# A 1x1 convolution of two by two blocks, made by seven products instead of eight

## The chip, the cores and the metric

The kernel runs on one core of a Trainium2 chip. Time is device time in microseconds (us) from start to end of one execution. TensorE (PE) multiplies, VectorE (DVE) and ScalarE (ACT) work elementwise, GpSimd (POOL) and SyncE (SP) mostly issue transfers. Each engine takes its instructions strictly in the order in which the program lists them, and waits at an instruction until what it needs is there. PE writes its results to PSUM, which the kernel uses as banks that it hands round ("big", 128 x 1024 numbers each), and reads its operands from SBUF. ACT computes silu and exp from tables; going from one function to the other needs an ACT_TABLE_LOAD.

## The reference, cut to what matters

```python
t = cbs(x, cv1_w, cv1_bn, 0)             # 1x1 convolution, batch norm, silu
ys = [t[:, :C], t[:, C:]]                # C = 256 channels of 32x32
for i in range(2):                       # two bottlenecks
    yi = ys[-1]
    z = cbs(yi, m_cv1_w[i], m_cv1_bn[i], 1)              # 3x3
    z = bot_attention(z, m_qkv_w[i], m_rw[i], m_rh[i])   # 4 heads of 64
    z = silu(bn_eval(conv2d(z, m_cv2_w[i], 0), m_cv2_bn[i]))   # this is m2
    ys.append(yi + z)
return cbs(concatenate(ys, axis=1), cv2_w, cv2_bn, 0)
```

The input (8 images of 512 channels) goes through a group norm first, and is added to the result at the end. All is 32-bit. m2 is the 1x1 convolution from 256 to 256 channels behind attention, with its batch norm, silu and the addition of `yi`.

## The kernel before, in words

The eight images are worked off in four pairs (p = 0 to 3, images a and b), each pair through cv1, the two bottlenecks (n = 0 and 1) and cv2. A 1x1 convolution of 256 channels on 1024 positions is a product of two by two blocks: two blocks of 128 input channels (k), two of 128 output channels (oc), two halves of 512 positions (half). One product of a 128x128 weight with a 128x512 block is two matmul instructions in the trace. Many convolutions of the kernel are already made in Strassen's way (in Winograd's form), by seven products and sums of blocks: the projection to q, k and v (`project_strassen`, L939) with its products named `11`, `s1`, `12`, `s4`, `s2`, `s3`, `22` and its sums on DVE, and pieces of cv1 (`nxt.begin`, `rest`, `adds`, `finish`).

`m2` (L1328 to L1345) isn't: it makes eight products (L1336), each pair of them adding up in PSUM, four silus straight from PSUM (L517, `t<-m_ps`), and four additions of `yi` on DVE (L1344). It is called 16 times: for each pair, bottleneck and image. Its weights `m2_sb` for both bottlenecks are loaded once at the start.

The calls for image a, which the change touches, stand at three kinds of places:

- *direct*: p = 0, n = 0. m2 runs, and behind it the rest of cv1 and a projection made in the plain way.
- *more*: n = 0 of p = 1 and 2. m2 stands between the pieces `nxt.rest(0)` to `nxt.rest(3)` of the next image's cv1 (x_ps, L1828; copies L1839 and L1842), and image b's projection follows.
- *middle*: n = 1 of every pair, and n = 0 of p = 3; five places. m2 is called inside image b's projection, by `middle()`, between its products `s2` and `s3`.

At a middle place the order of before is: `end.spread()` and `end.scale()` (L1195 scales attention's output z, two instructions on DVE; the second is the block that m2's products of k = 1 wait for), m2's eight products, the projection's `s3` and `22` (L958 for q and k, L964 for v), their additions on DVE (L1033 to L1050), and then attention: four groups of logits (L1082), each into a bank of PSUM that an exp (L1086) empties, then the products with v (L1119), and sums of the exps on DVE (L1100, L1103). In n = 1 of p = 1 and 2 `middle()` also calls `nxt.finish()`, which puts six silus of the next cv1 (`ypad`, `y_half`) on ACT behind m2's four, and `nxt.keep()`. Behind all of these `exp_table()` (L532, a table load and a tiny activation `spare`) is put behind the last silu, and the exps follow. DVE's and ACT's order is the order in which the program issues, apart from `tc.issue_after`, which puts an instruction behind a named one.

## Time and profile before

| | us |
|---|---|
| median of 3 runs (lowest, highest) | 2207.69 (2206.78, 2208.18) |
| the profiled execution | 2206.25 |
| its span in the profile | 2204.8 |
| PE busy | 2176.4 |
| DVE busy | 1817.5 |
| ACT busy | 1094.1 |

The profiled execution took 2206.25 us, of which the profile's span covers 2204.8; the other 1.45 lie around it. A busy time is the time in which an engine's instructions ran, summed up. In the lists of instructions each row is: start, duration, engine, line, operation, output <- inputs, shapes, how many, and in brackets the idle time ahead of it and what ended it.

### The profile page before, as it was taken

How to read it: one execution, taken by the hardware profiler on the slowest of the kernel's cores; microseconds unless marked ns; L12 is line 12 of the kernel's file. 1: busy time of each engine (PE TensorE's matmuls, PEld its weight loads, DVE VectorE, ACT ScalarE, POOL GpSimd, SP SyncE). 2: the span in 40 equal slices, each digit the busy share in tenths (PEclk: the TensorE clock that was granted, in tenths of full speed). 3: DMA queues.
4: the chain of work that ended last, by engine and by line, in shares of the span. 5: the costliest groups of instructions: out<-in, count | busy, mean ns of one | idle time of the engine just before them, and what ended most of it. 6: DMA issues, size and time to landing. Idle time of an engine off the chain costs nothing.

```text
span 2204.8 us, 40989 instructions
## 1 busy us (share of the span) xinstructions
PE 2176.4 (99%) x16546; PEld 1117.9 (51%) x16546; DVE 1817.5 (82%) x2996; ACT 1094.1 (50%) x1320; POOL 220.9 (10%) x393
## 2 busy tenths in 40 slices
PE   7999999999999999999999999999999999999998
PEld 3653438343484444734458443564346834383436
DVE  8988879878978688986897868997788877897677
ACT  7454553554225666366314676455622465336543
POOL 4322210000210000000012000000002100000001
PEclk9999999999999999999999999999999999999999
DMA  9954447212583323612159141542126811261224
GB/s 276 323 159 143 163 149 262 84 52 74 153 287 95 118 84 127 208 51 77 57 135 330 33 165 38 184 140 78 59 68 170 301 30 45 92 204 32 76 59 116
DMA packets 135529, 291.93 MB, mean 132 GB/s; under 512 B 33732, under 2 KB 61376, under 8 KB 134308
## 3 DMA queue, kind: packets, MB, share of 16 engines
q1 hardware_dynamic: 102708, 201.01, 27.4%
q0 software_dynamic: 32624, 88.23, 13.6%
q8 instruction: 132, 2.16, 0.4%
q14 instruction: 65, 0.53, 0.1%
HBM read 219.58 MB, written 69.60 MB: 131 GB/s over the span
## 4 chain that ended last, share of the span: by engine, by line
PE 87%; DVE 8%; DMA 2%; issue 1%; ACT 1%; POOL 0%; SPq 0%; DVEq 0%; ACTq 0%; POOLq 0%
PE av_ps L1119 19%; PE l_ps L1082 18%; PE c_ps L675 10%; PE p_ps L958 7%; PE c L1356 5%; PE m_ps L1336 5%; PE c_q L1404 5%; PE x_ps L1828 4%; PE ps L545 3%; PE c L1388 3%; PE p_ps L964 3%; PE c_new L1356 2%; PE s_ps L1137 1%; DMA taps<-in_m_cv_w_dram 1%; DVE acc L1103 1%
## 5 line engine op out<-in xcount | busy, mean ns | idle before, releaser
L1086 ACT ACTIVATE pt<-l_ps 128x1024 f32<-128x1024 f32 x512 | 495.6, 1023 | 328.2 <-PE l_ps L1082 252.4
L1082 PE MATMUL l_ps<-q,kr 64*64 64x512 f32 x4096 | 485.5, 590 | 0.9 <-ACT pt L1086 0.9
L1119 PE MATMUL av_ps<-pt,vT 64*64 64x512 f32 x4096 | 484.7, 590 | 1.2 <-DVE z L1127 1.1
L1103 DVE TENSOR_TENSOR acc<-acc,pt 128x1024 f32<-128x1024 f32 x362 | 442.5, 1222 | 37.2 <-ACT pt L1086 9.8
L1119 PEld LDWEIGHTS av_ps<-pt,vT 64*64 64x64 f32 x4096 | 156.0, 133 | 280.7 <-issue 234.8
L1082 PEld LDWEIGHTS l_ps<-q,kr 64*64 64x64 f32 x4096 | 157.4, 133 | 270.3 <-issue 246.4
L675 PE MATMUL c_ps<-v_in,u 128*64 128x128 f32 x4320 | 238.5, 273 | 0.0
L675 PEld LDWEIGHTS c_ps<-v_in,u 128*64 128x64 f32 x4320 | 235.8, 137 | 4.9 <-issue 4.6
L1127 DVE TENSOR_TENSOR z<-av_ps,z 128x512 f32<-128x512 f32 x64 | 43.9, 687 | 98.6 <-ACT z L1126 98.5
L1336 PE MATMUL m_ps<-z,m_sb 128*128 128x512 f32 x256 | 114.2, 593 | 0.4 <-DVE z L1195 0.4
L958 PE MATMUL p_ps<-t_z,sq 128*128 128x512 f32 x224 | 105.9, 595 | 0.0
L680 ACT COPY c_m<-c_ps 128x512 f32<-128x512 f32 x48 | 28.1, 586 | 151.0 <-PE c_ps L675 132.7
L517 ACT ACTIVATE t<-m_ps,bh,sh 128x512 f32<-128x512 f32 x64 | 46.3, 774 | 95.4 <-PE m_ps L1336 94.2
L1100 DVE TENSOR_TENSOR acc<-pt 128x1024 f32<-128x1024 f32 x64 | 78.0, 1219 | 14.2 <-PE s_ps L1137 8.7
L958 PE MATMUL p_ps<-z,sq 128*128 128x512 f32 x168 | 81.3, 604 | 0.8 <-ACT z L517 0.7
L1336 PEld LDWEIGHTS m_ps<-z,m_sb 128*128 128x128 f32 x256 | 47.7, 190 | 57.4 <-issue 52.3
L1504 POOL DMA_DIRECT2D c_out<-in_x_dram x48 | 43.4, 1041 | 273.6 <-ACT c_out L517 271.9
L1195 DVE TENSOR_TENSOR z<-z,rs 128x512 f32<-128x512 f32 x64 | 42.2, 685 | 30.0 <-DMA rs<-r_dram 29.9
L517 ACT ACTIVATE z<-z,bh,sh 128x512 f32<-128x512 f32 x64 | 48.7, 809 | 25.2 <-DVE z L737 25.1
L958 PEld LDWEIGHTS p_ps<-t_z,sq 128*128 128x128 f32 x224 | 39.5, 191 | 36.6 <-issue 34.4
L517 ACT ACTIVATE c_out<-c,bh,sh 128x512 f32<-128x512 f32 x12 | 14.0, 1280 | 85.7 <-PE c L1388 77.7
L1828 PE MATMUL x_ps<-t_x,sw 128*128 128x512 f32 x128 | 55.9, 592 | 0.0
(409 smaller groups left out, 3326.7 us busy)
## 6 DMA issues: line engine op xcount, KB each, us to landing
u<-u SPq DMA_DIRECT2D x135, 512.0 KB
y_in<-y SPq DMA_DIRECT2D x32, 512.0 KB
rs<-r_dram SPq DMA_DIRECT2D x126, 128.0 KB
sq<-sq SPq DMA_DIRECT2D x42, 384.0 KB
x<-in_x_dram SPq DMA_DIRECT2D x28, 512.0 KB
r_in<-r SPq DMA_DIRECT2D x28, 512.0 KB
c_out<-in_x_dram POOLq DMA_DIRECT2D x56, 256.0 KB, 6.4
out_dram<-c_out POOLq DMA_DIRECT2D x56, 256.0 KB, 5.4
```

The costliest lines, as they stand in the source:

```text
L517: silued[0] = nc.scalar.activation(dst, src, AF.Silu, scale=sh[:, k : k + 1], bias=bh[:, k : k + 1])
L675: conv_product[0] = nc.tensor.matmul(to[o], us[cp][:, k, row, c, o], rhs, start=(k == 0), stop=(k == NM - 1),)
L958: nc.tensor.matmul(ps[:, o, :], w[:, o, :], rhs, start=not onto, stop=True, skip_group_check=onto)
L1082: nc.tensor.matmul(ps[kh * HD : (kh + 1) * HD, hd, :], kr[r, c, o : o + HD], q[r, c, ts(half, HALF)], start=True, stop=True,)
L1086: last_exp[0] = exp = nc.scalar.activation(pt, ps, AF.Exp, scale=SCALE)
L1100: return nc.vector.tensor_tensor(accs[g], pt[0], pt[1], ALU.add)
L1103: ins = nc.vector.tensor_tensor(accs[g], accs[g], pt[i], ALU.add)
L1119: nc.tensor.matmul(avs[g][hd * HD : (hd + 1) * HD, kh, :], vT[r, j, o : o + HD], pt[i][r, hd, :], start=(j == 0), stop=(j == NJ - 1),)
L1336: nc.tensor.matmul(pss[half][:, oc, :], m2_sb[:, n, k, ts(oc, P)], ao[:, k, ts(half, HALF)], start=(k == 0), stop=(k == NM - 1),)
L1356: nc.tensor.matmul(ps[:, o, :], w[:, k, ts(o, P)], rhs[part][:, c], start=(k == 0 and not onto), stop=(k == KB - 1), skip_group_check=onto,)
L1404: nc.tensor.matmul(to, a[:, c], b[:, c], start=first and c == 0, stop=last and c == 1, skip_group_check=True)
L1828: nc.tensor.matmul(ps[:, o, :], w[:, c, ts(o, P)], rhs[c], start=(c == 0 and not onto), stop=(c == 1), skip_group_check=onto,)
```

## The change

For image a, `m2` becomes `m2_by_seven`, in three steps that the caller puts at different points. With b11, b12 (k = 0) and b21, b22 (k = 1) as blocks of z and eight 128x128 weights (four blocks, four sums of them):

- `begin`: t1 = b12 - b11; products `11`*b11 and `s1`*t1 into bank a; two copies of them on ACT (u, m5). These need only the k = 0 blocks, so they stand ahead of the last scaling.
- `sums`, behind the last scaling: t2, t3, t4 on DVE.
- `finish`: `12`*b21 and `s4`*b22 onto bank a, `s2`*t2 and `s3`*t3 into bank e, `22`*t4 into bank f; on DVE u += e0, c12 = a1 + u, u += e1, m5 += u, u -= f; silus of a0 (from PSUM), c12, m5 and u (from SBUF); four additions of `yi`.

At the middle places `begin` and `sums` are in `middle`, and `finish` in a new call-back `end`, which the projection calls behind its v2. `nxt.finish()`, `nxt.keep()` and `exp_table()` go with it. At the places *more*, `begin` stands between `rest(0)` and `rest(1)`, and `finish` behind `rest(1)`. The weights are no longer kept: `load_m2` loads them before each bottleneck into one buffer, with the sums from pair 1 on; in pair 0 `make_m2` makes the sums on DVE and stores them. Image b keeps eight products.

```diff
-    m2_sb = const.tile([P, N, NM, C], F32, name="m2_sb")
...
+    def load_m2(n, sums=False):
+        w = const.tile([P, 8, P], F32, tag="m2_sb", name="m2_sb")
+        for o in range(NM):
+            nc.sync.dma_start(
+                w[:, NM * o : NM * (o + 1)], m_cv2_w[n].rearrange("(k p) o -> p k o", p=P)[:, :, ts(o, P)]
+            )
+        if sums:
+            nc.sync.dma_start(w[:, 4:], m2_dram[n])
+        return w
...
-            tt(v2, v_of(ps_w[:, 1]), v_of(u_v), ALU.add)
+            last = tt(v2, v_of(ps_w[:, 1]), v_of(u_v), ALU.add)
+            if end:
+                with tc.issue_after(last.ins):
+                    end()
...
+            def begin():
+                t12 = acc_room("t_w", [P, 2, HALF])
+                a = ps_big.tile([P, 2, HALF], F32, tag="big", name="m2_ps")
+                mm(a[:, 0], "11", b11)
+                tt(t12[:, 0], b12, b11, ALU.subtract)
+                mm(a[:, 1], "s1", t12[:, 0])
+                u, m5 = room("rs"), room("rs")
+                nc.scalar.copy(u, a[:, 0])
+                nc.scalar.copy(m5, a[:, 1])
+                kept.extend((t12[:, 0], t12[:, 1], a, u, m5))
...
+            def finish(behind=None, apart=True):
+                _, t2, a, u, m5, t3, t4 = kept
+                mm(a[:, 0], "12", b21, True)
+                mm(a[:, 1], "s4", b22, True)
+                e = ps_big.tile([P, 2, HALF], F32, tag="big", name="m2_ps")
+                mm(e[:, 0], "s2", t2)
+                mm(e[:, 1], "s3", t3)
+                c11, c12 = room("t"), room("t")
+                put(c11, a[:, 0], 0)
+                last = tt(u, e[:, 0], u, ALU.add)
...
+                if apart:
+                    f = ps_big.tile([P, 2, HALF], F32, tag="big", name="m2_ps")
+                    add_12()
+                    freed[0] = tt(u, e[:, 1], u, ALU.add)
...
+                mm(f[:, 0], "22", t4)
+                tt(m5, u, m5, ALU.add)
+                put(m5, m5, 1)
+                last = tt(u, u, f[:, 0], ALU.subtract)
+                put(u, u, 1)
+                if behind:
+                    with tc.issue_after(last.ins):
+                        behind()
+                for t, oc, half in ((c11, 0, 0), (c12, 0, 1), (m5, 1, 1), (u, 1, 0)):
+                    with tc.issue_after(freed[0].ins):
+                        last = tt(dst_of(oc, half), img(t), inner(yi, oc, half), ALU.add)
+                return last
...
         def middle():
             end.spread()
-            end.scale()
-            s.m2(1, z[:, :, 0], Y2[0], lambda oc, half: img(y3a[half][:, oc, :]))
+            m2_a.begin()
+            with tc.issue_after(end.scale().ins):
+                m2_a.sums()
+
+        def finish_m2():
+            m2_a.finish()
             if more:
                 nxt.finish()
                 nxt.keep()
             s.exp_table()
```

How the order moves. The lines of the changed file are up to 95 higher than those of before (L517 is L530 there, L532 L545, L1033 L1046, L1040 and L1041 L1056 and L1057, L1086 L1102, L1195 L1211, L1842 L1935, L1000 L1013). PE's order at a middle place is now: products `11` and `s1` of m2, the projection's `s3` (q, k, then v), `12`, `s4`, `s2`, `s3`, `22` of m2, the projection's `22` (v, then q and k), logits.

DVE at the middle place of p = 1, n = 1, before, from the scaling to the second of the two additions that finish k and q for the third group of logits (`t` are m2's silus, `kr`, `q`, `vT` the projection's outputs):

```order
L1195 TENSOR_TENSOR z<-z,rs 128x512 x2
L1344 TENSOR_TENSOR y_half<-t,ypad_67 128x512 x4
L1033 TENSOR_TENSOR kr<-p_ps,u_z 128x512
L1034 TENSOR_TENSOR q<-p_ps,u_z 128x512
L1035 TENSOR_TENSOR vT<-p_ps,u_zv 128x4x128
L1038 TENSOR_TENSOR kr<-kr,m_z 128x512
L1039 TENSOR_TENSOR q<-q,m_z 128x512
L1040 TENSOR_TENSOR kr<-kr,p_ps 128x512
L1041 TENSOR_TENSOR q<-q,p_ps 128x512
```

and now, from the last of the projection's first five additions (L1055 is the former L1039; `w_kept` are u and m5, `t` at L1393 is c12):

```order
L1055 TENSOR_TENSOR q<-q,m_z 128x512
L1390 TENSOR_TENSOR w_kept<-m_ps,w_kept 128x512
L1393 TENSOR_TENSOR t<-m_ps,w_kept 128x512
L1399 TENSOR_TENSOR w_kept<-m_ps,w_kept 128x512
L1417 TENSOR_TENSOR y_half<-t,ypad_67 128x512
L1408 TENSOR_TENSOR w_kept<-w_kept 128x512
L1417 TENSOR_TENSOR y_half<-t,ypad_67 128x512
L1410 TENSOR_TENSOR w_kept<-w_kept,m_ps 128x512
L1417 TENSOR_TENSOR y_half<-w_kept,ypad_67 128x512
L1056 TENSOR_TENSOR kr<-kr,p_ps 128x512
L1417 TENSOR_TENSOR y_half<-w_kept,ypad_67 128x512
L1057 TENSOR_TENSOR q<-q,p_ps 128x512
```

m2's four additions stood ahead of the projection's; now five additions of m2's own and the four of `yi` stand behind the projection's first five, and L1056 and L1057 among them and behind them.

ACT at the same place, before, from m2's silus to the first exps:

```order
L517 ACTIVATE t<-m_ps,bh,sh 128x512 x4
L517 ACTIVATE ypad_64<-ypad_64,bh,sh 128x16x32 x4
L517 ACTIVATE y_half<-y_half,bh,sh 128x512 x2
L532 ACT_TABLE_LOAD
L532 ACTIVATE spare<-zero 128x1
L1086 ACTIVATE pt<-l_ps 128x1024 x10
```

and now:

```order
L1368 COPY w_kept<-m_ps 128x512
L1369 COPY w_kept<-m_ps 128x512
L530 ACTIVATE t<-m_ps,bh,sh 128x512
L530 ACTIVATE t<-t,bh,sh 128x512
L530 ACTIVATE w_kept<-w_kept,bh,sh 128x512 x2
L530 ACTIVATE ypad_64<-ypad_64,bh,sh 128x16x32 x4
L530 ACTIVATE y_half<-y_half,bh,sh 128x512 x2
L545 ACT_TABLE_LOAD
L545 ACTIVATE spare<-zero 128x1
L1102 ACTIVATE pt<-l_ps 128x1024 x10
```

The silus of c12, m5 and u (rows `t<-t` and `w_kept<-w_kept`) read what DVE has made; the six silus of the next cv1, the table load and the exps stand behind them as before.

ACT at the place p = 1, n = 0, before, from the copies of x_ps ahead of m2's silus to the copy of u_z for image b's projection:

```order
L1839 COPY x_kept<-x_ps 128x32x8x4 x2
L517 ACTIVATE t<-m_ps,bh,sh 128x512 x4
L517 ACTIVATE y_half<-y_half,bh,sh 128x512 x2
L532 ACT_TABLE_LOAD
L532 ACTIVATE spare<-zero 128x1
L1842 COPY ypad_61<-x_ps 128x16x8x4 x4
L1000 COPY u_z<-p_ps 128x1024
```

and now:

```order
L1932 COPY x_kept<-x_ps 128x32x8x4
L530 ACTIVATE t<-m_ps,bh,sh 128x512
L530 ACTIVATE t<-t,bh,sh 128x512
L530 ACTIVATE w_kept<-w_kept,bh,sh 128x512 x2
L1935 COPY ypad_61<-x_ps 128x16x8x4 x2
L530 ACTIVATE y_half<-y_half,bh,sh 128x512 x2
L1935 COPY ypad_61<-x_ps 128x16x8x4 x2
L545 ACT_TABLE_LOAD
L545 ACTIVATE spare<-zero 128x1
L1013 COPY u_z<-p_ps 128x1024
```

The exp table's load stood ahead of the four copies to `ypad`; now it stands behind them, ahead of the copy of u_z.

## Prediction

> **What bounds the kernel now.** I read the page's busy times first, then TensorE's (PE's) waits, then the timeline around the calls of m2.

> ```profile
> span 2204.8 us, 40989 instructions
> PE 2176.4 (99%) x16546; PEld 1117.9 (51%) x16546; DVE 1817.5 (82%) x2996; ACT 1094.1 (50%) x1320; POOL 220.9 (10%) x393
> L1336 PE MATMUL m_ps<-z,m_sb 128*128 128x512 f32 x256 | 114.2, 593 | 0.4 <-DVE z L1195 0.4
> ```
> ```profile
> PE gm_ps L760 <- DVE mv L754: 7.9, 1, 7.9
> PE l_ps L1082 <- ACT pt L1086: 0.9, 2, 0.5
> ```

> PE is busy 2176.4 of 2204.8 us, so 28.4 us of idle time are left in all, and the longest single wait is 7.9 us, at the start. Work taken off PE is therefore worth its time, as long as nothing else becomes late; there is almost no idle PE time in which new lateness could hide. One row is a warning: twice the logits (L1082) already wait for an exp, 0.9 us in all.

> What a product of m2 costs on PE stands in the chain of waits:

> ```profile
> 754.94 6.87 PE m_ps L1336 x16
> ...
> 856.26 6.87 PE m_ps L1336 x16
> ```

> One call is 16 matmul instructions (eight products, each two instructions) in 6.87 us: 0.859 us a product. Matmuls overlap, so the mean of 593 ns in the group is not the price of one.

> The timeline at the "middle" places (m2 of the first image inside the projection of the second) shows what follows m2 there. This is PE in pair 0, bottleneck 1:

> ```profile
> 458.71 1.88 PE L1336 MATMUL m_ps<-z,m_sb 128*128 128x512 f32 x4
> ...
> 470.89 3.66 PE L1082 MATMUL l_ps<-q,kr 64*64 64x512 f32 x32
> 474.37 1.04 PE L1119 MATMUL av_ps<-pt,vT 64*64 64x512 f32 x8
> ```

> m2 begins at S = 458.71, the logits at S+12.18, and four groups of eight logit matmuls pass without a stop. In pair 1, bottleneck 1, the fourth group does stop:

> ```profile
> 998.41 1.88 PE L1336 MATMUL m_ps<-z,m_sb 128*128 128x512 f32 x4
> ...
> 1010.59 2.81 PE L1082 MATMUL l_ps<-q,kr 64*64 64x512 f32 x24
> 1013.86 1.09 PE L1082 MATMUL l_ps<-q,kr 64*64 64x512 f32 x8 [0.46 <-ACT pt L1086]
> ```

> Three groups have PSUM room; the fourth needs the bank of the first, and starts when the first exp has emptied it. ScalarE (ACT) in the same stretch shows why that exp is late:

> ```profile
> 1005.70 1.45 ACT L517 ACTIVATE t<-m_ps,bh,sh 128x512 f32<-128x512 f32 x2 [1.13 <-PE m_ps L1336]
> 1007.04 2.92 ACT L517 ACTIVATE ypad<-ypad,bh,sh 128x512 f32<-128x512 f32 x4
> 1009.87 1.51 ACT L517 ACTIVATE y_half<-y_half,bh,sh 128x512 f32<-128x512 f32 x2
> 1011.39 1.28 ACT L532 ACT_TABLE_LOAD   x1
> 1012.69 0.20 ACT L532 ACTIVATE spare<-zero 128x1 f32<-128x1 f32 x1
> 1012.80 1.92 ACT L1086 ACTIVATE pt<-l_ps 128x1024 f32<-128x1024 f32 x2
> ```

> Behind m2's last silu stand six silus of the next projection (1007.04 to 1011.39, 4.35 us), then the exp table (1.41 us from 1011.39 to the exp at 1012.80), then the exps. So the end of m2's last silu sets the first exp, and the first exp sets PE. There is no room left: PE waits 0.46 us for it already. The question of this case is when m2's last silu ends afterwards.

> **The change part by part.** Removed: one product in each of eight calls, 8 x 0.859 = 6.9 us of PE. All of it is path, as PE is.

> Added, at each of the eight places: two copies on ACT (`u`, `m5`), and on VectorE (DVE) four sums of blocks and five additions behind products. DVE's pace:

> ```profile
> 1007.79 0.69 DVE L1033 TENSOR_TENSOR kr<-p_ps,u_z 128x512 f32<-128x512 f32 x1
> 1008.39 0.68 DVE L1034 TENSOR_TENSOR q<-p_ps,u_z 128x512 f32<-128x512 f32 x1
> ```

> starts lie 0.60 us apart; nine more operations are 5.4 us a place. What matters is that the last two silus of m2 now take their input from the end of a DVE chain, instead of from PSUM directly.

> *Five middle places* (all bottleneck 1, and bottleneck 0 of the last pair). Where the scaling ends, in pair 0 and in pair 1:

> ```profile
> 459.75 1.28 DVE L1195 TENSOR_TENSOR z<-z,rs 128x512 f32<-128x512 f32 x2
> ```
> ```profile
> 1000.73 0.69 DVE L1195 TENSOR_TENSOR z<-z,rs 128x512 f32<-128x512 f32 x1 [0.59 <-DMA rs<-r_dram]
> ```

> That is S+2.32 in pair 0; in pair 1 it is S+3.01, for a DMA that came late. I walk the new order from S. PE, at 0.859 us a product: `11` and `s1` to 1.72, qk and v of the projection's s3 to 4.30, `12` and `s4` to 6.02, `s2` and `s3` to 7.74, `22` to 8.60, v and qk of the projection's 22 to 11.18, where the logits could start, 1.0 earlier than the 12.18 of before (0.86 of it the product). DVE, at 0.60: the last scaling ends at 2.32; `t2`, `t3`, `t4` run to 4.2, the projection's five additions (L1033 to L1039) to 7.2; then, in queue order, u+e0 from 7.95 (when its product is there), c12, u+e1, one addition to y, m5, another, and u-f at 11.67 to 12.35. L1040 and L1041, which finish k and q for the later logits, stand behind that, L1041 ending near 14.75; so the third group of logits can go at 14.8 only. ACT: the silu of `u` runs from 12.4 to 13.2 (0.73 to 0.8 us each by the row at 1005.70). Before it ended at S+8.74.

> Where the exp table follows directly (pair 0, and both bottlenecks of pair 3: three places) the first exp comes at 13.2 + 1.41 = 14.6, takes 0.96 (1.92 for two), and the fourth group starts 0.1 behind it at about 15.75, where it was at 12.18 + 3 x 0.86 = 14.76: 1.0 late, and a little more because one sum of exps is now queued ahead of the last additions to k. I take +1.1 each, +3.3 in all. Bounds: -0.86, if the silu ends early enough to hide, and +2, if DVE's chain is a further three operations late.

> Where the six silus stand between (bottleneck 1 of pairs 1 and 2: two places), the first exp comes at 13.2 + 4.35 + 1.41 = 18.96 and the fourth group at about 20.0; before it was at 1013.86 - 998.41 = 15.45. That is +4.6 each, +9.2 in all: PE has nothing else in its order to do meanwhile. Bounds: +2.8 if the chain runs three operations ahead of my walk, +5.8 with two more behind.

> The table's price of 1.41 us is the row's. [...]

> *Bottleneck 0 of pairs 1 and 2* (two places, m2 between pieces of the next pair's first projection). ACT there, before:

> ```profile
> 764.72 1.28 ACT L532 ACT_TABLE_LOAD   x1
> ...
> 768.71 1.97 ACT L1842 COPY ypad<-x_ps 128x512 f32<-128x512 f32 x2 [0.65 <-PE x_ps L1828]
> 770.45 1.08 ACT L1000 COPY u_z<-p_ps 128x1024 f32<-128x1024 f32 x1
> 771.55 1.28 ACT L517 ACT_TABLE_LOAD   x1
> 773.02 2.93 ACT L517 ACTIVATE ypad<-ypad,bh,sh 128x512 f32<-128x512 f32 x4 [0.19 <-DVE ypad L1894]
> 775.86 0.99 ACT L1001 COPY m_z<-p_ps 128x1024 f32<-128x1024 f32 x1
> ```

> The load at 764.72 ran in time that ACT spent waiting for x_ps. In the new order it stands behind all four copies to ypad, right ahead of the u_z copy, as the silus of m2 end later. So u_z goes from 770.45 to about 772.1, and the silus and the m_z copy move with it, by some 1.45. PE waits for that copy:

> ```profile
> 777.16 1.02 PE L958 MATMUL p_ps<-z,sq 128*128 128x512 f32 x2
> ```

> begins 0.3 behind m_z's end. The product saved brings PE there 0.86 sooner and it waits longer; I take +1.1 each, +2.2 in all (bounds -0.86, if the copies also come that much sooner and cover the load, and +1.9).

> *Bottleneck 0 of pair 0* (direct): the product saved is 0.86, but the next projection takes the bank of `a`, which is free after c12 = a1 + u, a DVE addition behind the first silu and u+e0. By the same prices that ends 6.9 after m2's start, when eight products ended before. I take 0 (bounds -0.86 and +0.9).

> *Weights.* m2's weights and their sums are now loaded before each bottleneck, into one buffer that the previous call frees. By the chain's rows pair 1 is done with the buffer at 856.26 + 6.87 = 863.1 and needs the next weights at 998.4: 135 us for a load. What stands behind it on SyncE's queue waits for that last product too, but not for longer. In pair 0 four small sums on DVE for each bottleneck, and a store on GpSimd's queue, lie in an attention. I take nothing; if the cover were gone, PE would wait for the rest of a load, and by the 0.59 us that the late DMA above cost, eight places would give up to 4.7.

> Sum: 3.3 + 9.2 + 2.2 + 0 = +14.7. Against the profiled execution's 2206.25 (span 2204.8 and 1.45 around it) that gives 2220.95; the median of the runs, 2207.69, lies 1.44 above, and 2207.69 + 14.7 = 2222.4. I say 2222.

> **The rivals.**

> *It works as meant.* 8 x 0.859 = 6.9 comes off: 2200.8. This needs the late silus to be hidden at every place; for the middle places the last silu would have to end by about S+12.2 where the table follows, and by S+8.7 where six silus do. For it: PE's busy share, and 0.86 us a place that is certainly gone. Against: the 0.46 us at 1013.86 says that the cover at two places is already used up. Chance 0.07.

> *Only the two places with the six silus pay.* If the other six keep their product, -6 x 0.859 = -5.2 stands against +9.2: +4.0, 2211.7. It is decided by whether DVE reaches u-f about 1.2 us earlier than I walk it, and by the table load in pairs 1 and 2. Chance 0.08.

> *The PE clock falls in the longer waits.* At the two worst places PE would stand still for about 4.6 us.

> ```profile
> 0.00:10.00 10.00, 0.76 (x8) 0.64 (x8) 4.22 (x13) 2.20 (x4) 2.11 (x19) 1.00 0.76 258
> 10.00:20.00 10.00, 7.94 (x18) 3.43 (x19) 9.61 (x27) 8.78 (x19) 1.08 (x2) 1.00 0.86 218
> ...
> 2200.00:2205.00 5.00, 0.00 (x0) 0.00 (x0) 0.00 (x0) 0.00 (x0) 0.00 (x0) 0.53 0.15 43
> ```

> The granted clock (third figure from the end) is 1.00 in the first 20 us although PE idles for 9.2 of the first ten, and 0.53 in the last five, in which PE does nothing. So it can fall within a few us of idling, and did not at the start. Were it at half for as long as a stall lasts, some 3.4 us of following work would take 1.7 more at each place: +3.4, 2225.8. [...] Chance 0.1.

> *DVE's backlog does not go away.* DVE is at 82%, and gets 5.4 us more at each place, just ahead of attention's sums of exps. If a third of that came out on PE at all eight places, 8 x 1.8 = 14.4 would be added: 2237. Its idle share of 18% speaks against. Chance 0.06.

> **How the numbers follow.** The forecast itself has 0.69. Its range by the terms: low 3 x 0.3 + 2 x 3.6 - 2 x 0.86 = +6.4, high 3 x 2 + 2 x 5.6 + 2 x 1.9 = +21, that is 2214 to 2229; low goes to 2212 to come close to the second rival, and 2229 holds the clock's case. Outside are the first rival (0.07), the last (0.06) and the lower half of the second (0.04). What a measurement of this kernel can tell from no change is 0.2%, 4.4 us. Faster by more: the first rival, 0.07. Within: most of the second, 0.07. Slower: the rest, 0.86.

> **What would show it.** Right: at the two places with the six silus the fourth group of logits waits 4 to 5 us for an exp, and PE's waits have a row l_ps <- ACT pt of some 9 to 13 us with a longest of about 4.5; the exp table's load lies some 4.5 us later from the start of m2 than before; the last silu of m2 comes 12 to 13 us after the first product; PE's busy time falls by about 7 us all the same. Wrong: l_ps waits of under 1 us with the same order; a last silu before S+10; a longer span with no new waits (then the clock or DVE); a load of m2's weights that PE waits for.

## The result, and the profile after

The changed kernel takes 2231.89 us (median of 4 runs, 2230.28 to 2232.03) where the kernel before takes 2207.91 (4 runs beside it): 24.0 us more, a ratio of 1.0108 (95% interval 1.009 to 1.0125). The profiled execution took 2231.86, its span 2230.4. The forecast had the direction and most of the places, and its range ended at 2229.

The page and PE's waits after:

```profile
span 2230.4 us, 41113 instructions
PE 2181.1 (98%) x16530; PEld 1118.2 (50%) x16530; DVE 1863.5 (84%) x3076; ACT 1104.0 (50%) x1336; POOL 221.5 (10%) x395
```
```profile
PE l_ps L1098 <- ACT pt L1102: 8.0, 2, 4.0
PE l_ps L1098 <- DVE q L1057: 6.5, 5, 1.3
...
PE p_ps L971 <- ACT m_z L1014: 2.9, 2, 1.4
...
PE p_ps L971 <- ACT u_z L1013: 0.7, 2, 0.4
...
PE p_ps L971 <- DVE z L1143: 0.6, 1, 0.6
PE ps L558 <- DVE t L1393: 0.6, 1, 0.6
```

The wait of the logits for an exp was 0.9 us in two pieces and is 8.0 in two. Five waits for q are new (1.3 each, one at each middle place), and so are those for the copies m_z and u_z at the two places of bottleneck 0. PE's busy time should have fallen by 6.9 with eight products fewer, and has risen by 4.7: a first sign that PE ran slower for a while, though not the whole of it. In the first experiment below, where the clock stays up, it is 2175.5, only 0.9 under the kernel before; where the other 6 stay is not shown.

ACT at the place of pair 1, bottleneck 1 (m2's first product starts at 1004.63):

```profile
1010.87 0.78 ACT L530 ACTIVATE t<-m_ps,bh,sh 128x512 f32<-128x512 f32 x1 [3.25 <-PE m_ps L1353]
1014.59 0.81 ACT L530 ACTIVATE t<-t,bh,sh 128x512 f32<-128x512 f32 x1 [2.94 <-DVE t L1393]
1016.52 0.81 ACT L530 ACTIVATE w_kept<-w_kept,bh,sh 128x512 f32<-128x512 f32 x1 [1.11 <-DVE w_kept L1408]
1017.72 0.81 ACT L530 ACTIVATE w_kept<-w_kept,bh,sh 128x512 f32<-128x512 f32 x1 [0.39 <-DVE w_kept L1410]
1018.44 2.92 ACT L530 ACTIVATE ypad<-ypad,bh,sh 128x512 f32<-128x512 f32 x4
1021.26 1.50 ACT L530 ACTIVATE y_half<-y_half,bh,sh 128x512 f32<-128x512 f32 x2
1022.78 1.28 ACT L545 ACT_TABLE_LOAD   x1
1024.08 0.20 ACT L545 ACTIVATE spare<-zero 128x1 f32<-128x1 f32 x1
1024.18 2.83 ACT L1102 ACTIVATE pt<-l_ps 128x1024 f32<-128x1024 f32 x3
```

and PE there:

```profile
1017.74 1.09 PE L1098 MATMUL l_ps<-q,kr 64*64 64x512 f32 x8
1020.14 1.09 PE L1098 MATMUL l_ps<-q,kr 64*64 64x512 f32 x8 [1.31 <-DVE q L1057]
1025.24 1.98 PE L1098 MATMUL l_ps<-q,kr 64*64 64x512 f32 x8 [4.02 <-ACT pt L1102]
1027.00 1.59 PE L1135 MATMUL av_ps<-pt,vT 64*64 64x512 f32 x8
```

The last three silus of m2 wait for DVE (2.94, 1.11, 0.39), nothing passes them in ACT's queue, and the six silus, the table and the exps come out behind them: the six start 13.81 us behind m2's first product, and 2.88 behind it where the first experiment puts them ahead. The eight logits at 1025.24 take 1.98 where those at 1020.14 take 1.09. That is the clock:

```profile
1020.00:1025.00 5.00, 1.09 (x8) 0.21 (x8) 3.87 (x7) 4.97 (x7) 1.10 (x2) 0.97 0.45 185
1025.00:1030.00 5.00, 4.76 (x32) 1.62 (x36) 3.66 (x4) 3.04 (x4) 0.00 (x0) 0.69 0.34 133
1567.00:1572.00 5.00, 1.09 (x8) 0.21 (x8) 4.07 (x7) 4.97 (x8) 1.10 (x2) 0.88 0.44 180
1572.00:1577.00 5.00, 4.56 (x24) 1.53 (x28) 3.46 (x3) 3.24 (x4) 0.00 (x0) 0.50 0.34 134
1577.00:1582.00 5.00, 5.00 (x48) 1.53 (x46) 3.51 (x5) 1.94 (x2) 0.00 (x0) 0.93 0.01 3
```

These are stretches of 5 us with the granted clock third from the end: 0.69 and 0.50 right behind the two waits of 4 us. The trace's clock records give 0.50 from 1024.71 to 1028.13 and from 1570.85 to 1577.67, and otherwise 1.00 from the first record (17.78) to 4 us before the end.

To see where the 25.6 us of span came from, I matched the two traces by the products with v (L1119, as many in every kernel): how much later the 200th of image b's attention starts than before, less the same for image a's attention ahead of it, is what a place costs. In us against the kernel before; "to there" is the start of the program up to the first attention:

| kernel | to there | p0 n0 | p0 n1 | p1 n0 | p1 n1 | p2 n0 | p2 n1 | p3 n0 | p3 n1 |
|---|---|---|---|---|---|---|---|---|---|
| predicted | 0 | 0 | 1.1 | 1.1 | 4.6 | 1.1 | 4.6 | 1.1 | 1.1 |
| changed | 1.68 | 0.69 | 2.13 | 1.66 | 6.57 | 1.63 | 7.67 | 1.91 | 1.53 |
| silus first | 0.14 | 0.69 | 2.12 | 1.68 | 0.91 | 1.66 | 0.74 | 1.55 | 1.53 |
| PE kept awake | 2.11 | 0.68 | 2.13 | 1.66 | 4.76 | 1.65 | 4.66 | 1.51 | 1.53 |
| eight at middle | 2.50 | 0.68 | 0.70 | 1.67 | 0.00 | 1.66 | -0.10 | 0.01 | 0.00 |
| weights reloaded | 0.15 | 0.01 | 0.70 | 0.02 | 0.00 | 0.01 | -0.10 | 0.00 | 0.00 |
| no table | 2.13 | 0.68 | 2.12 | -0.30 | 7.03 | -0.34 | 7.66 | 1.51 | 1.60 |
| additions late | 0.06 | 0.69 | 2.01 | 1.66 | 5.92 | 1.65 | 5.71 | 1.65 | 0.35 |
| all three | 0.23 | 0.69 | 2.01 | -0.31 | 0.06 | -0.35 | -0.09 | 2.48 | 0.34 |
| finish in the middle | 1.30 | 0.70 | 2.12 | -0.31 | 0.12 | 0.02 | 0.03 | 1.74 | -0.24 |
| before, no table | 0.12 | 0.01 | 0.01 | 1.49 | 0.00 | 1.85 | 0.01 | 0.01 | 0.00 |
| two places alone | 2.71 | 0.00 | 0.01 | -0.30 | 0.00 | -0.31 | -0.10 | 0.01 | 0.00 |

Elsewhere two traces differ by under 1 us. The start differs by up to 2.7 between kernels that do nearly the same work there (the first two experiments do the same as the change, and have 0.14 and 2.11); it is no part of the change, and goes at least in part with the clock (last section).

### The profile page after: what moved, and what is told of

It is laid out like the page before. It is cut to its first block, busy times and chain, and to the rows that moved or that the text cites. A ratio compares the mean times of both kernels' runs of the same rounds, so it can differ in the third digit from the quotient of the medians.

```text
span 2230.4 us, 41113 instructions
## 1 busy us (share of the span) xinstructions
PE 2181.1 (98%) x16530; PEld 1118.2 (50%) x16530; DVE 1863.5 (84%) x3076; ACT 1104.0 (50%) x1336; POOL 221.5 (10%) x395
## 3 DMA queue, kind: packets, MB, share of 16 engines
q0 software_dynamic: 32784, 88.75, 13.5%
## 4 chain that ended last, share of the span: by engine, by line
PE 80%; DVE 13%; ACT 3%; DMA 2%; issue 1%; SPq 0%; POOL 0%; DVEq 0%; ACTq 0%
PE av_ps L1135 18%; PE l_ps L1098 17%; PE c_ps L688 10%; PE c L1449 5%; PE c_q L1497 5%; PE p_ps L971 5%; PE ps L558 4%; PE x_ps L1921 4%; PE c L1481 3%; PE m_ps L1429 2%; PE c_new L1449 2%; PE p_ps L977 2%; DVE acc L1119 2%; PE m_ps L1353 1%; PE s_ps L1153 1%
## 5 line engine op out<-in xcount | busy, mean ns | idle before, releaser
L1102 ACT ACTIVATE pt<-l_ps 128x1024 f32<-128x1024 f32 x512 | 495.7, 1023 | 320.3 <-PE l_ps L1098 242.1
L1119 DVE TENSOR_TENSOR acc<-acc,pt 128x1024 f32<-128x1024 f32 x362 | 442.7, 1223 | 39.1 <-ACT pt L1102 12.2
L1211 DVE TENSOR_TENSOR z<-z,rs 128x512 f32<-128x512 f32 x64 | 42.4, 687 | 31.6 <-DMA rs<-r_dram 31.6
L530 ACT ACTIVATE z<-z,bh,sh 128x512 f32<-128x512 f32 x64 | 48.7, 809 | 25.4 <-DVE z L750 25.2
L530 ACT ACTIVATE t<-m_ps,bh,sh 128x512 f32<-128x512 f32 x40 | 29.4, 774 | 58.3 <-PE m_ps L1429 38.5
L1429 PE MATMUL m_ps<-z,m_sb 128*128 128x512 f32 x128 | 57.1, 594 | 0.6 <-DVE z L1211 0.6
L530 ACT ACTIVATE c_out<-c,bh,sh 128x512 f32<-128x512 f32 x12 | 14.0, 1275 | 85.7 <-PE c L1481 77.7
L977 PEld LDWEIGHTS p_ps<-sq,z 128*128 128x128 f32 x336 | 43.6, 191 | 20.7 <-issue 13.7
```

Of the source, the lines that this page charges most:

```text
L530: silued[0] = nc.scalar.activation(dst, src, AF.Silu, scale=sh[:, k : k + 1], bias=bh[:, k : k + 1])
L1102: last_exp[0] = exp = nc.scalar.activation(pt, ps, AF.Exp, scale=SCALE)
L1119: ins = nc.vector.tensor_tensor(accs[g], accs[g], pt[i], ALU.add)
L1429: nc.tensor.matmul(pss[half][:, oc, :], w[:, NM * oc + k], ao[:, k, ts(half, HALF)], start=(k == 0), stop=(k == NM - 1),)
```

## The experiments

My theory: m2's silus now wait for a chain on DVE, ACT's queue carries that lateness to the exps, and the longest waits bring the clock down as well. The rivals: DVE has too much to do, in whatever order; or the reloaded weights cost. All experiments are edits of the changed kernel, if nothing else is said. Times are medians, with the ratio to runs of the kernel before beside them, whose medians were 2207.2 to 2207.7.

**Six silus first.** The finish of the next cv1 is called ahead of m2's, and its silus are tied to the copy of m5:

```diff
+            if more:
+                nxt.finish()
+                nxt.keep()
             m2_a.finish()
-            if more:
-                nxt.finish()
-                nxt.keep()
             s.exp_table()
...
-                nc.scalar.copy(m5, a[:, 1])
+                m2_silu[0] = nc.scalar.copy(m5, a[:, 1])
```

> In bottleneck 1 of pairs 1 and 2 the six silus of the next cv1 stand ahead of m2's silus on ScalarE (behind the copy of m5), and no longer behind them. The theory of the queue (the last silu of m2 waits for VectorE's chain, and what stands behind it waits too): the 4.0 us that the logits wait for an exp at these two places go, the clock stays at 1.00, and each costs 1.5 to 2 us as the other middle places do, where it cost 6.5 and 7.7: about 10.8 less, 2221. The rival, that VectorE's added work is what delays the logits (6.5 us of waits for q): at or above 2229, since VectorE's order is the same.

2217.10 us (ratio 1.0045, 1.0028 to 1.0062), 14.8 less than the change. ACT and PE of it, pair 1, bottleneck 1 (m2's first product starts at 1003.09):

```profile
1005.97 2.93 ACT L530 ACTIVATE ypad<-ypad,bh,sh 128x512 f32<-128x512 f32 x4
1008.81 1.51 ACT L530 ACTIVATE y_half<-y_half,bh,sh 128x512 f32<-128x512 f32 x2
...
1015.85 0.81 ACT L530 ACTIVATE w_kept<-w_kept,bh,sh 128x512 f32<-128x512 f32 x1 [0.38 <-DVE w_kept L1410]
1016.68 1.28 ACT L545 ACT_TABLE_LOAD   x1
...
1018.09 2.83 ACT L1102 ACTIVATE pt<-l_ps 128x1024 f32<-128x1024 f32 x3
```
```profile
1018.27 1.97 PE L1098 MATMUL l_ps<-q,kr 64*64 64x512 f32 x16 [1.31 <-DVE q L1057]
1020.05 1.90 PE L1135 MATMUL av_ps<-pt,vT 64*64 64x512 f32 x16
```

The six silus run in time in which ACT waited for DVE anyway. The wait for an exp is gone, the one for q stays, the clock is 1.00, and the two places cost 0.91 and 0.74 instead of 6.57 and 7.67. That is less than the 1.5 to 2 that I expected, and the start was 1.5 shorter in this execution, so the time lies 4 below the expected 2221. What was queued behind the late silus was thus 12.6 us of the loss, the clock's share in it. That these two now cost less than the plain ones fits the 0.46 us that PE waited at each before.

**PE kept awake.** Four products whose results are overwritten, between the third and the fourth group of logits at the two worst places:

```diff
+                    if awake and pair is pairs[1] and i == 1:
+                        avs[0] = ps_av.tile([P, 2, HALF], F32, tag="av", name="av_ps")
+                        for _ in range(awake):
+                            nc.tensor.matmul(avs[0][:, 0, :], kr[:, 0, 0:P], q[:, 0, 0:HALF], start=True, stop=True)
```

> Everything as in the changed kernel, with four extra products (128x128 by 128x512, 3.4 us, results overwritten) between the third and the fourth group of logits at the two worst places, so that TensorE works through most of its 4 us wait. If the half clock there (3.4 and 6.8 us at 0.5) comes from TensorE standing still, the clock stays at 1.00 and the products behind the wait run at full speed: about 4.6 less, 2227.3, with the fourth group at the same time as before. If the half clock has another cause, 2231.9 and the same rows of 0.5.

2225.54 (1.0081, 1.0064 to 1.0098). PE of it, and the clock:

```profile
1020.15 1.09 PE L1102 MATMUL l_ps<-q,kr 64*64 64x512 f32 x8 [1.31 <-DVE q L1057]
1021.57 3.67 PE L1094 MATMUL av_ps<-q,kr 128*128 128x512 f32 x8 [0.33 <-DVE vT L1060]
1025.26 1.09 PE L1102 MATMUL l_ps<-q,kr 64*64 64x512 f32 x8
1026.17 1.90 PE L1139 MATMUL av_ps<-pt,vT 64*64 64x512 f32 x16
```
```profile
1025.00:1030.00 5.00, 4.98 (x45) 1.74 (x48) 3.64 (x4) 3.96 (x6) 0.00 (x0) 1.00 0.34 138
...
1572.00:1577.00 5.00, 5.00 (x52) 1.80 (x48) 4.79 (x6) 3.03 (x4) 0.00 (x0) 1.00 0.01 3
```

The fourth group starts when it did (1025.26 against 1025.24), and takes 1.09 instead of 1.98. Useless work made the kernel faster: by 1.81 at one place (6.57 to 4.76) and 3.01 at the other (7.67 to 4.66), 4.8 in all. The median fell by 6.3, more than these two; in the profiled executions the rest lies in differences of under 1 us elsewhere.

**Eight products at the middle places.** `middle` is the one of before, and calls m2 of before with the loaded weights; the other three places keep seven.

```diff
             end.spread()
-            m2_a.begin()
-            with tc.issue_after(end.scale().ins):
-                m2_a.sums()
-
-        def finish_m2():
-            m2_a.finish()
+            end.scale()
+            s.m2(1, m2_w, z[:, :, 0], Y2[0], lambda oc, half: img(y3a[half][:, oc, :]))
```

> m2 of the first image has eight products again at the five middle places, and seven at the other three; weights as in the changed kernel. If the middle places are the cost, the drift between the two traces there (1.5, 6.5, 7.7, 2.0 and 1.5, 19.2 in all) goes: 2212.7. If the loss lies in the weights' loads, pair 0's sums or VectorE's load as a whole, more than 2220.

2212.48 (1.002, 1.0011 to 1.003). The middle places are back to nothing, but for 0.70 in pair 0.

**The weights reloaded, nothing else.** The kernel before, eight products everywhere, with `load_m2` and `make_m2` of the change.

```diff
-    for n in range(N):
-        load_m2(n)
+    m2_w = load_m2(0)
...
+        m2_w = load_m2(1, p > 0)
...
+            behind[3] = lambda: make_m2(1, m2_w)
```

> The kernel before with eight products everywhere, but with the changed kernel's way with m2's weights: one buffer, loaded before each bottleneck with the sums, which pair 0 makes and stores (the sums aren't used). If the loads are hidden, as the prediction took: 2207.9, within 1. If they are a part of the 3.1 us by which the changed kernel was late ahead of pair 0's bottleneck 1: 2209 to 2211.

2206.32 (0.9996, 0.9986 to 1.0006): the loads cost nothing that can be measured. One place shows in the trace, 0.70 in pair 0, bottleneck 1, where the four sums of weights are made on DVE just ahead of the sums of exps that end an attention; PE then waits 0.6 for the last piece of z:

```profile
440.01 0.29 DVE L244 TENSOR_TENSOR m_sb<-m_sb 128x128 f32<-128x128 f32 x1
...
440.95 5.21 DVE L1116 TENSOR_TENSOR acc<-acc,pt 128x1024 f32<-128x1024 f32 x4
...
447.40 0.68 DVE L1140 TENSOR_TENSOR z<-av_ps,z 128x512 f32<-128x512 f32 x1
```

In the last experiment, which makes no sums for bottleneck 1, that place is at 0.01.

**No exp table at the two places of bottleneck 0.**

```diff
             nxt.finish()
             nxt.keep()
-            s.exp_table()
             feed(cv1_keys(1))
```

> The changed kernel without the call for the exp table ahead of image b's projection in bottleneck 0 of pairs 1 and 2 (the table is loaded there, changed back for silus 3 us later, and loaded once more ahead of the exps anyway). If the load's place between the copies to ypad and the copy of u_z is what PE waits for there (3.6 us of waits for m_z and u_z in all), those waits go and each place costs nothing or gains its product: 2227 to 2228.7. If the copies are late because m2's silus are, 2231 or more.

2228.22 (1.0098, 1.0083 to 1.0114): 3.7 less than the change. Both places go from +1.66 and +1.63 to -0.30 and -0.34, and PE's waits for m_z and u_z are gone. The edit also let the copy of m_z go ahead of the four silus in ACT's order, so the two effects aren't apart.

**The same in the kernel before.**

> The kernel before without the same call for the exp table. Its second load there was followed by a wait of PE for m_z, 0.25 to 0.4 us at each of two places: 2207 by the waits. If the load was hidden altogether: 2207.7.

2210.96 (1.0016, 1.0007 to 1.0025): slower by about 3.5, where I expected a little less or nothing; 1.49 and 1.85 of it are at the two places. ACT and PE of it:

```profile
770.64 1.05 ACT L1000 COPY u_z<-p_ps 128x1024 f32<-128x1024 f32 x1
773.01 2.93 ACT L517 ACTIVATE ypad<-ypad,bh,sh 128x512 f32<-128x512 f32 x4 [1.32 <-DVE ypad L1894]
775.85 0.99 ACT L1001 COPY m_z<-p_ps 128x1024 f32<-128x1024 f32 x1
```
```profile
776.89 1.12 PE L958 MATMUL p_ps<-z,sq 128*128 128x512 f32 x2 [1.11 <-ACT m_z L1001]
```

The silus start when they did (773.01 against 773.02), as they wait for DVE's ypad; the second load had stood in time that was free. And without the loads the order of the projection's products changed as well: one with z, which needs the bank that m_z empties, now stands ahead of those with t_z, and waits 1.11. This run therefore doesn't price the table, it prices another order.

**The additions of yi late.** At the middle places `finish` returns its four additions, and the projection issues them behind its last:

```diff
                 projected[0] = tt(q1, q1, u[:, 0], ALU.add)
+            if end:
+                add_yi(projected[0])
```

> The changed kernel with the four additions of yi at the five middle places behind the projection's last addition on VectorE, and no longer between m2's own and the projection's. The last silu's input then comes 1.2 us sooner, and q for the third group of logits 1.8 sooner. If VectorE's order is what these places wait for: the five waits for q (6.5 us) go, the three plain places cost about 0 where they cost 1.5 to 2, the two others 1.2 less each: 2225. If it is the number of VectorE's operations, which stays the same: 2231.9.

2227.38 (1.0093, 1.0078 to 1.0109), profiled at 2225.12. PE's waits:

```profile
PE l_ps L1100 <- ACT pt L1104: 12.5, 5, 5.0
...
PE av_ps L1137 <- DVE z L1145: 3.3, 5, 1.1
```

The five waits for q are gone. In their place the logits wait for an exp at all five places, a little less, and at two places of them DVE is late at the end of the next group: products with v wait up to 1.1 for z, where before no such wait was over 0.5. So p3 n1 fell from 1.53 to 0.35, while p0 n1 and p3 n0 hardly moved: 2227.4 lies between what I expected of the order (2225) and of the number of operations (2231.9). The order was a part of the cost; at p0 n1 and p3 n0 the lateness only moved to another wait.

**All three edits.**

> The three edits together: six silus ahead of m2's, the additions of yi late, no exp table at the two places. By the queues every middle place then starts its fourth group of logits within 0.3 of the kernel before (first exp at 13.6 us from m2's start, fourth group at 14.65 where it was at 14.76), and the other places gain up to a product: 2206 to 2208, so seven products are worth almost nothing at the middle places even when nothing is queued wrongly. If the saved products are all worth their time once the queues are mended: 2200.8 to 2203.

2210.52 (1.0016, 1.0007 to 1.0025), above the 2206 to 2208 expected. The two worst places are at 0.06 and -0.09, the two of bottleneck 0 at -0.31 and -0.35; but p0 n1 and p3 n0 still cost 2.01 and 2.48. The logits still wait 0.8 for an exp at each of the five middle places.

**m2 whole, ahead of the projection's s3.** `finish` is called in `middle` again, in its form with one bank less; silus first, three additions late, no table.

```diff
                 m2_a.sums()
+            if more:
+                nxt.finish()
+                nxt.keep()
+            kept_adds.append(m2_a.finish(apart=False, in_t=False, late=True))
+            s.exp_table()
```

> Seven products at all eight places, with the whole of m2 (its finish too) ahead of the projection's s3 on PE and VectorE at the five middle places, as the eight stood before; the six silus behind the copy of m5; three of the four additions of yi behind the projection's last; no exp table at the two places of bottleneck 0. The last silu of m2 should then end 10.7 us after m2's first product (13.5 in the changed kernel, 8.7 before), and the fourth group of logits come at 14.4. If the places cost what the order of the queues makes them cost, the two worst ones gain up to 1 each, the plain ones 0.4, less what VectorE's backlog gives back later (about 1 at bottleneck 1 of pair 0 and bottleneck 0 of pair 3, as with the late additions): 2206 to 2208. If VectorE's added work costs whatever its order: 2210 and more.

2211.54 (1.0018, 1.0009 to 1.0027): not the 2206 to 2208 by my theory, but what the rival gave. In pair 0 m2's last silu ended 11.4 us after its first product (10.7 expected), and the waits for exps came down to 1.0 us in all. What stays is DVE:

```profile
PE av_ps L1137 <- DVE z L1145: 4.6, 5, 1.8
```

At p0 n1 and p3 n0 a wait for z in the attention behind takes back what the place gains. So for these two places the rival (DVE's added work costs in any order that I tried) stands; at the other three middle places it doesn't: 0.12, 0.03 and -0.24.

The trace of before shows a difference between the two places and the others. These are the first 20 us of the attention behind the place, at p0 n1 and, by contrast, at p1 n1 (the third pair of figures is DVE):

```profile
474.00:494.00 20.00, 20.00 (x192) 7.04 (x188) 19.31 (x20) 12.22 (x13) 1.09 (x2) 1.00 0.14 54
1015.00:1035.00 20.00, 20.00 (x192) 7.05 (x188) 16.30 (x17) 12.03 (x14) 0.00 (x0) 1.00 0.11 44
```

DVE is busy for 19.31 and, at p3 n0, 19.34 of the 20 us, so there is no room in which to catch up; at p1 n1, p2 n1 and p3 n1 it is busy for 16.30, 16.30 and 17.06. This fits all five places, but no run varies DVE's room by itself.

**Seven products only where they gain.** At the two places of bottleneck 0, without the table; eight elsewhere.

```diff
-                m2_a.begin()
-                m2_a.sums()
-                last = m2_a.finish(apart=False)
+                last = s.m2(0, m2_w, z[:, :, 0], Y1[0], lambda oc, half: inner(Y2[0], oc, half))
...
-        m2_w = load_m2(1, p > 0)
+        m2_w = load_m2(1)
```

> Seven products only at the two places in bottleneck 0 of pairs 1 and 2, without the exp table's load there, and eight everywhere else; sums of weights for bottleneck 0 alone. By the places of the earlier runs (-0.30 and -0.34 there without the load, 0 elsewhere): 0.6 below the kernel before, 2207, which can't be told from it. If a saved product were worth its 0.86 there: 1.7 below, hardly more.

2208.27 (1.0002, 0.9993 to 1.0011): the same as before, as expected; -0.30 at each of the two places. No version that I ran is faster than the kernel before by more than its runs differ.

## Why the prediction was right in direction and wrong in size

The profiled span grew by 25.6. The eight places make 23.8 of it, 1.68 is the start. The forecast's sum was 14.7. The top of its range, 2229, was added up without the clock; it held the clock only on top of the sum itself (2225.8), not on top of other terms that came out large as well, and both happened.

- *The queue at the two worst places: right.* With the clock held up, they cost 4.76 and 4.66; forecast 4.6 each. The walk holds step by step in pair 1: m2's last silu ends at S+13.9 (1018.53; the walk had 13.2), the first exp starts at S+19.55 (18.96), the fourth group at S+20.6 (20.0).
- *The clock: the step that failed.* "The granted clock (third figure from the end) is 1.00 in the first 20 us although PE idles for 9.2 of the first ten": from this I gave the rival 0.1 and left it out of the sum. It came about and cost 4.8 (forecast for that case 3.4). The reading was wrong, and the trace of before could have told: its first clock record is at 15.76 us, and ahead of it the view prints 1.00 because there is no record. The first matmuls behind that idle time stand so:

```profile
12.06 6.38 PE L545 MATMUL ps<-x,w_cols 128*128 128x512 f32 x10 [2.49 <-ACT x L822]
18.37 0.28 PE L760 MATMUL gm_ps<-mv,gmat 64*64 64x2 f32 x4
18.58 2.84 PE L545 MATMUL ps<-x,w_cols 128*128 128x512 f32 x6
```

Six take 2.84, so ten should take 4.6 (four more at 0.43), and took 6.38: PE did run slower behind the wait, though the clock's figure said 1.00. Taken one by one, the starts of these ten lie 0.85 apart between 13.07 and 15.63 and 0.43 apart from 16.13 on. No row of before shows the 3.4 us of half clock that this rival's sum used. At these two places the changed kernel's clock was at 0.50 for 3.41 and 6.83 us, behind waits of 4.02, and the loss was 1.81 and 3.01 us, where the sum had 1.7 each.
- *The plain middle places: chain right, the wait another, too small.* Forecast 1.1 each, measured 1.43 (p0 n1 without the 0.70 of the sums), 1.91 and 1.53. The price was that of the fourth group waiting for an exp (S+15.75; the terms given for it add up to 15.67). What PE waits for there is q, for the third group. The walk had this wait, ending at S+14.8, but gave it no price; it ended at S+15.1 in pair 0 and at S+15.5 in pair 1 (1020.14). With the additions late it goes, and a wait of 0.8 for an exp takes its place; that brought p3 n1 down by 1.2 and the other two hardly.
- *The table: right by the row.* In the changed kernel the load starts at 1022.78 and the exp at 1024.18, 1.40 later.
- *Bottleneck 0 of pairs 1 and 2: mechanism right, too small.* 1.66 and 1.63 for 1.1; u_z and m_z are waited for as forecast, and both waits go with the table's load.
- *The direct place:* 0.69 where I took 0. The wait for c12 (0.6) is the one forecast, and eats the saved product: image b's projection starts 6.91 after m2's first product, where it was 6.86. Most of the 0.69 comes behind it, at a wait for z in the attention.
- *The weights: almost right.* No load was waited for; the sums of pair 0, taken at nothing, cost 0.70.

Of the sum's shortfall of 9.1 at the places, the clock is 4.8, the plain places 1.6, bottleneck 0 of pairs 1 and 2 1.1, and pair 0 1.4 (0.69 and 0.70); the two worst places without the clock are 0.2 of it. Of the signs named ahead, the fall of PE's busy time by some 7 us did not come, not even with the clock up, and the waits of the logits for an exp are 8.0 us in all, under the 9 to 13 forecast.

## What to carry to other kernels

Fewer products on the bound engine are a gain only if their results leave it as soon as before: look at what stands behind the last reader of the result in each queue, and put what doesn't depend on it ahead (12.6 us here, by moving six silus). A wait of TensorE of some 4 us cost more than itself here (1.81 and 3.01 us more); count the half clock behind it (3.41 and 6.83 us at 0.50 here), and judge the clock in a trace by how long equal instructions take, not by the clock's figure alone. An edit that only takes an instruction away can change the scheduler's order elsewhere: compare the order before reading the time as that instruction's price.

## What the runs showed of the hardware that I had not expected

Two waits of the same length, 4.02 us, were followed by half clocks of 3.41 us at one place and 6.83 at the other in the same execution; the loss was 1.81 and 3.01. Filling the wait with useless products kept the clock at 1.00. With PE kept awake, 3.41 us of half clock stand near 83 us as well, behind a wait of 2.02 for v_in, and with two places alone the clock was 0.83 over the ten us from 80; the start was 2.11 and 2.71 us longer there. The kernel before and the changed kernel have the same wait, 2.03 in both, and a clock of 1.00 behind it. So a wait of 2 us was followed by half a clock in some executions and not in others. The mean clock of the changed kernel's four runs differed too, from 0.995 to 0.997.

```profile
79.22:82.64 3.42, 1.70 (x32) 1.46 (x28) 3.38 (x8) 0.16 (x1) 0.00 (x0) 1.00 1.02 347
...
79.88:83.30 3.42, 1.40 (x26) 1.24 (x24) 3.42 (x11) 0.00 (x0) 0.86 (x1) 1.00 1.01 345
83.30:86.71 3.41, 3.41 (x36) 3.41 (x34) 3.41 (x7) 2.92 (x5) 0.38 (x2) 0.50 1.01 370
...
1567.44:1570.85 3.41, 0.99 (x8) 0.10 (x8) 3.34 (x6) 3.39 (x5) 1.10 (x2) 1.00 0.27 115
1570.85:1574.26 3.41, 1.82 (x12) 0.61 (x16) 1.22 (x2) 3.35 (x5) 0.00 (x0) 0.50 0.86 346
1574.26:1577.67 3.41, 3.41 (x24) 0.98 (x20) 3.20 (x4) 1.02 (x1) 0.00 (x0) 0.50 0.02 5
```

The wait of 2.0 near 81 us lay across a window's end in the changed kernel, with 1.71 us in the first window, and inside one window where PE was kept awake. The wait of 4.02 at 1567 gave 2.42 us to one window and 1.59 to the next, so the clock fell and came back only a window later; the one at 1021 filled a window and left 0.53 to the next, so it came back at once. How much these waits cost beyond themselves thus hung on where the windows lay. At the start, the steps between the first ten large products fall from 0.85 to 0.43 us at the first clock record, which came at 15.76 us in the kernel before and at 17.78 in the changed kernel; the ten took 6.38 and 7.31 us, 0.93 of the 1.68 by which the changed kernel's start was longer. The ends of PE's rows are modelled, so the idle times are those of these traces; no run moved a wait on purpose.
